# A convolution's totals moved to ScalarE, and two residual sums moved into a TensorE bank, in a hybrid scan kernel

## The chip, the cores and the metric

The kernel runs on one core of one Trainium2 chip. The metric is the device time in microseconds of one execution. PE is TensorE's matmul side and PEld its weight loads, DVE is VectorE, ACT is ScalarE, POOL is GpSimd, SP is SyncE, which issues the DMAs. L769 means line 769 of the kernel before.

## The reference

Eight images of 96 channels by 64x64 pixels pass through two layers. The first is a state-space block with a channel-attention convolution; the second is a linear attention and a feed-forward with rounded numbers. What matters here, cut:

```python
# layer 0, x: (b, 64, 64, 96)
xc = silu(depthwise3x3(in_proj(ln(x))) + conv_b)          # 192 channels
ys = selective_scan(...)          # 4 directions, 16 states, 4096 steps: h = exp(dt*A)*h + dt*u*B; y = C.h
x  = x * skip_scale + out_proj(ln(y) * silu(z))
h  = conv3x3(gelu(conv3x3(ln(x)) + cab1_b)) + cab2_b
a  = sigmoid(relu(h.mean((2, 3)) @ ca1_w.T + ca1_b) @ ca2_w.T + ca2_b)
x  = x * skip_scale2 + h * a
# layer 1, t: tokens of 96
t = t + (q k^T v)(ln(t)) @ Wff + bff                      # no softmax: one matrix per image
t = t + q_acc(q_acc(W2 @ q_mul(relu(q_acc(q_acc(W1 @ q_mul(ln(t))) + b1)))) + b2)
```

`q_mul` rounds to an 8-bit float, `q_acc` to a 16-bit one.

## The kernel before

An image is cut into 8 chunks of T = 512 pixels; a tile is channels by 512. The main loop is the scan. Its `units` are image by pixel order by direction by chunk, 32 to an image, 256 in all. A unit has 24 slots. In each slot ACT makes one 128x512 tile of decays into a bank (`decays`, L1062), two slots ahead; DVE runs one scan over it (L1123) and, in a bit over half of the slots, the product with C (L1125); ACT copies the last column out for the next chunk (the `carry` copies, L1126 and L1131). POOL makes the inputs of four slots at a time (`inputs`, L946, 128x2048) and the products with C that DVE doesn't (`outputs`, L952). PE adds the states up (`sums`, L972), ACT evicts the sum (`gather`, L992). `nat`, `ua`, `ub` (L919 to L928) are the step sizes; `delta`, `du`, `b`, `c` come by DMA on SP's queue.

Instructions stand on each engine in the order in which the Python program issues them (a schedule written out by hand); `plan` names the slot of each step of the scan.

Everything else is run as side work from the same loop. `advance` is called at the end of each slot: it moves `clock` on by one, issues the DMAs that are due (`later` puts one HOLD = 3 slots on), and lets each side stream run one step. A step is a generator that issues some instructions and yields for how many slots it rests: `yield PA` is two slots, for a matmul to end before its eviction is issued; `landed` waits LAND = 11 slots from a fetch. There are two streams: `front` of the next image (kit `f0`), and `back_end` of the image before (kit `f1`), whose stages run in turn: `gated`, `first_conv`, `second_conv`, `channel_gate`, `attention`, `joined`, `feed_forward`. Image 0's units have no back end beside them. After the last unit the back end of image 7, apart from its first stage, runs alone, its chunks dealt to four kits (`f1`, `f0`, `y01`, `y2`): this is the tail. A kit has one bank, `bank(k.tag, ...)`, so each new use of it waits for the eviction of the last.

The stages that the change touches, per chunk:

- `second_conv`: three matmuls (L655) into the bank, ACT adds the bias and writes the tile `t` (L664), DVE sums `t` over its 512 columns into a column of `totals` (L666), and `t` is stored. `channel_gate` (L674) reads `totals` after the last chunk. One chunk's fetch is issued two chunks ahead (`nearer`).
- `feed_forward`: one matmul with the image's joined attention matrix `qkvf` (L767); DVE adds the bank, the bias `bff` and the residual tile `t` into `t` (L769); `norm` centres and scales (L376 to L382: centring matmul, ACT's square and copy, variance matmul, ACT's logarithm and exponential); DVE writes the 8-bit tile (L774); three times a matmul (L778), ACT's conversion and ReLU (L780, L781); ACT's 8-bit tile (L783); three matmuls (L787) with ACT's conversion to 16 bits and bias (L789, L790); POOL adds the result `o16` to `t` (L792), and `t` is stored to `out`.

In the trace an fp32 matmul stands as two records, an fp16 or fp8 one as one.

Of the kernel before, what the change touches and what calls it, by code (L numbers as in the profile page):

```python
# [10 lines left out]
F16 = mybir.dt.float16  # L11
F8 = mybir.dt.float8e5
AF = mybir.ActivationFunctionType
ALU = mybir.AluOpType
AX = mybir.AxisListType
# [4 lines left out]
B, C, HW = 8, 96, 64  # L20
# [18 lines left out]
PA = 2  # L39
# [4 lines left out]
def kernel(ctx: ExitStack, tc: tile.TileContext, a, out):  # L44
# [8 lines left out]
    nc = tc.nc  # L53
# [3 lines left out]
    wp = ctx.enter_context(tc.tile_pool(name="weights", bufs=1))  # L57
# [5 lines left out]
    def bank(tag, name):  # L63
        return psum.tile([P, T], F32, tag=tag, name=name, bufs=BANKS[tag])


    ident = wp.tile([P, P], F32, name="ident")
    make_identity(nc, ident)

    def const(shape, value, name):  # L70
        t = wp.tile(shape, F32, name=name)
        nc.vector.memset(t, value)
        return t
# [27 lines left out]
    for base, mult, step in ((0, 1, -16), (15, -1, 16)):  # L101
        nc.gpsimd.affine_select(
            out=heads, in_=heads, compare_op=ALU.is_ge, fill=0.0, base=base,
# [9 lines left out]
    def later(dst, src):  # L113

        requests.append((clock[0] + HOLD, dst, src))
# [7 lines left out]
    def load(name, shape):  # L123
        return into(wp.tile(shape, F32, name="w_" + name), a[name])
# [43 lines left out]
    cab2_b = load("cab2_b", [C, 1])  # L168
# [5 lines left out]
    wff, bff = load("wff", [C, C]), load("bff", [C, 1])  # L174
# [92 lines left out]
    totals = wp.tile([C, NC], F32, name="totals")  # L267
# [14 lines left out]
    def landed(*parts):  # L282
        while clock[0] < max(p.ready for p in parts):
            yield 1
# [87 lines left out]
    def norm(k, srcs, sq, d):  # L372

        ps = bank(k.tag, "ctr")[:C, :]
        for i, src in enumerate(srcs):
            nc.tensor.matmul(ps, cen_c, src, start=i == 0, stop=i == len(srcs) - 1)  # L376
        yield PA
        nc.scalar.activation(sq, ps, AF.Square)
        nc.scalar.copy(d, ps)  # L379
        yield 1  # L380
        ps = bank(k.tag, "var")[:C, :]
        nc.tensor.matmul(ps, ones_c, sq, start=True, stop=True)  # L382
        yield PA
        inv_std(ps, ps)
        yield 1
        return ps
# [140 lines left out]
    def back_end(b, s):  # L527
# [6 lines left out]
        small = {}  # L534
# [107 lines left out]
        def nearer(p, c):  # L642
            for dy in range(3):
                later(p.t[32 * dy : 32 * dy + 32], mid[:, 8 * c + dy : 8 * c + dy + 8, :])
            p.ready = clock[0] + LAND

        def second_conv(k, cs):
            if not k.solo:
                for p, c in zip(k.m3, cs):
                    nearer(p, c)  # L650
            for n, c in enumerate(cs):
                yield from landed(k.m3[n % 2])
                ps = bank(k.tag, "cab2")[:C, :]
                for dx in range(3):
                    nc.tensor.matmul(  # L655
                        ps, cab2_w[:, dx, :], k.m3[n % 2].t[:, :, dx : dx + HW], start=dx == 0, stop=dx == 2
                    )
                    if dx == 1:
                        yield 1
                yield PA  # L660
                if n + 2 < len(cs):
                    nearer(k.m3[n % 2], cs[n + 2])
                t = (k.s1, k.d1)[n % 2][:C]
                nc.scalar.activation(t, ps, AF.Identity, bias=cab2_b)  # L664
                yield 1
                nc.vector.tensor_reduce(totals[:, c : c + 1], t, AX.X, ALU.add)  # L666
                later(td[:, bass.ts(c, T)], t)
                if n == len(cs) - 1:
                    sources(k, cs[0])
                yield 1  # L670
# [25 lines left out]
        def sources(k, c):  # L696
            for part, src in ((k.ya, td), (k.za, x1d), (k.bs, s["base"])):
                fetch(part, src[:, bass.ts(c, T)])
# [41 lines left out]
        def normed_again(k, n, c):  # L740
            fetch(k.ln, lnd[:, bass.ts(c, T)])
            fetch(k.t2[n % 2], x1d[:, bass.ts(c, T)])
# [18 lines left out]
        def feed_forward(k, cs):  # L761

            for n, c in enumerate(cs):
                t = k.t2[n % 2].t[:C]
                yield from landed(k.ln, k.t2[n % 2])
                ps = bank(k.tag, "att")[:C, :]
                nc.tensor.matmul(ps, small["qkvf"], k.ln.t, start=True, stop=True)  # L767
                yield PA
                nc.vector.scalar_tensor_tensor(t, ps, bff, t, ALU.add, ALU.add)  # L769
                if n + 1 < len(cs):  # L770
                    normed_again(k, n + 1, cs[n + 1])
                yield 1
                rs = yield from norm(k, (t,), k.s1[:C], k.d1[:C])
                nc.vector.tensor_tensor(k.x8, k.d1[:C], rs, ALU.mult, saturate=False)  # L774
                yield 1
                for f in range(3):
                    ps = bank(k.tag, "ff1")
                    nc.tensor.matmul(ps, w1[:, bass.ts(f, P)], k.x8, start=True, stop=True)  # L778
                    yield PA
                    nc.scalar.copy(k.h16[:, f, :], ps)  # L780
                    nc.scalar.activation(k.h16[:, f, :], k.h16[:, f, :], AF.Relu, bias=b1[:, f : f + 1])  # L781
                    yield 1
                nc.scalar.activation(k.h8, k.h16, AF.Copy, saturate=False)  # L783
                yield 1
                ps = bank(k.tag, "ff2")[:C, :]
                for f in range(3):
                    nc.tensor.matmul(ps, w2[:, f, :], k.h8[:, f, :], start=f == 0, stop=f == 2)  # L787
                yield PA
                nc.scalar.copy(k.o16, ps)  # L789
                nc.scalar.activation(k.o16, k.o16, AF.Identity, bias=b2)  # L790
                yield 2
                nc.gpsimd.tensor_tensor(t, t, k.o16, ALU.add)  # L792
                later(out[b, :, bass.ts(c, T)], t)
                yield 1

        chunks = range(NC)[::-1]
        return (
            (gated, chunks), (first_conv, chunks[1::2]), (second_conv, chunks), (channel_gate, None),
            (attention, chunks), (joined, None), (feed_forward, chunks),
        )  # L800

# [423 lines left out]
```

## Time and profile before

| | |
|---|---|
| three runs: median (lowest to highest) | 11345.4 us (11343.77 to 11359.79) |
| the profiled execution: own time | 11372.37 us |
| its span | 11370.7 us |
| granted TensorE clock, share of full | 0.822 |
| first scan starts, last scan ends | 351.7 us, 11092.1 us |
| time of the 32 units of image 0 | 1287.8 us |
| of images 1 to 7 | 1351.2, 1351.7, 1348.8, 1348.3, 1348.2, 1348.3, 1356.1 us |

The profiled execution's own time is 1.7 us more than its span, and 27 us more than the median. Times inside it are told from the span's start. The times of units are taken from the start of their first scan on DVE. Image 0 has no back end beside its units, and images 1 to 6 have both streams, so that the difference of some 61 us is the price of the side work there; image 7 has a second `gated` beside its last units in place of the front stream.

The page gives for each engine the busy time, its share of the span and the count of instructions; a table of stretches gives the same for parts of the span. A group's row gives line, engine, operation, what is written from what, the count, then busy time, the mean in ns of one, and the idle time of the engine just before, with what ended it. Idle time of an engine that isn't the bound costs nothing.

### The profile page before, as it was taken

How to read it: one execution, taken by the hardware profiler on the slowest of the kernel's cores; microseconds unless marked ns; L12 is line 12 of the kernel's file. 1: busy time of each engine (PE TensorE's matmuls, PEld its weight loads, DVE VectorE, ACT ScalarE, POOL GpSimd, SP SyncE). 2: the span in 40 equal slices, each digit the busy share in tenths (PEclk: the TensorE clock that was granted, in tenths of full speed). 3: DMA queues.
4: the chain of work that ended last, by engine and by line, in shares of the span. 5: the costliest groups of instructions: out<-in, count | busy, mean ns of one | idle time of the engine just before them, and what ended most of it. 6: DMA issues, size and time to landing. Idle time of an engine off the chain costs nothing. (4 is left out here: it accounts for less than half of the span.)

```text
span 11370.7 us, 97041 instructions
## 1 busy us (share of the span) xinstructions
PE 8567.3 (75%) x23270; PEld 2328.5 (20%) x23270; DVE 10367.4 (91%) x10828; ACT 7508.4 (66%) x14939; POOL 10398.7 (91%) x2783
## 2 busy tenths in 40 slices
PE   6577657887778877888678876788768887676677
PEld 2111112222122211222112221222212221111122
DVE  0799999999999999999999999999999999999991
ACT  3566656767666676667766676666766667666674
POOL 0799999999999999999999999999999999999990
PEclk8678778888788877889778887888878888787787
DMA  2788878898888888888888888889888888888872
GB/s 71 171 197 197 201 189 210 209 225 196 203 210 212 219 198 202 210 215 215 195 207 210 216 214 194 210 205 228 202 200 211 212 220 195 198 198 195 201 188 78
DMA packets 1081039, 2253.24 MB, mean 198 GB/s; under 512 B 419609, under 2 KB 420314, under 8 KB 949395
## 3 DMA queue, kind: packets, MB, share of 16 engines
q1 hardware_dynamic: 1080467, 2247.05, 81.3%
q8 instruction: 184, 3.01, 0.1%
q14 instruction: 388, 3.18, 0.1%
HBM read 1507.14 MB, written 336.69 MB: 162 GB/s over the span
## 5 line engine op out<-in xcount | busy, mean ns | idle before, releaser
L946 POOL TENSOR_TENSOR hb<-b,du 128x2048 f32<-128x2048 f32 x1536 | 6939.0, 4535 | 21.3 <-DMA du<-ua 14.3
L1062 ACT ACTIVATE da<-delta,w_a_logs 128x512 f32<-128x512 f32 x6144 | 4216.7, 689 | 696.3 <-DVE hb L1123 575.8
L972 PE MATMUL p<-hb,halves 128*64 128x512 f32 x12288 | 3822.7, 731 | 800.1 <-POOL hb L952 382.1
L1123 DVE TENSOR_TENSOR_SCAN da<-da,carry,hb 128x512 f32<-128x512 f32 x3087 | 3949.0, 1279 | 58.0 <-ACT da L1062 54.3
L952 POOL TENSOR_TENSOR hb<-hb,c 128x2048 f32<-128x2048 f32 (+2 forms) x768 | 2984.9, 3887 | 304.7 <-ACT carry L1131 252.2
L1123 DVE TENSOR_TENSOR_SCAN hb<-da,carry,hb 128x512 f32<-128x512 f32 x2289 | 2781.0, 1264 | 57.7 <-ACT da L1062 56.7
L1125 DVE TENSOR_TENSOR hb<-da,c 128x512 f32<-128x512 f32 x3528 | 2440.5, 692 | 154.0 <-DVE da L1123 0.9
L1126 ACT COPY carry<-da 128x1 f32<-128x1 f32 x3528 | 554.9, 157 | 2351.6 <-DVE hb L1125 2341.1
L972 PEld LDWEIGHTS p<-hb,halves 128*64 128x64 f32 x12288 | 916.2, 161 | 3540.7 <-issue 2129.5
L434 PE MATMUL conv<-f0im,taps 97*128 97x512 f32 (+1 forms) x2088 | 903.5, 664 | 95.9 <-ACT f0pre L490 54.3
L928 POOL TENSOR_TENSOR ua<-nat,ua 128x512 f32<-128x512 f32 x256 | 327.3, 1279 | 257.5 <-DMA b<-xd 257.5
L1123 DVE TENSOR_TENSOR_SCAN da<-da,hb 128x512 f32<-128x512 f32 x441 | 537.7, 1219 | 26.0 <-POOL hb L946 24.6
L925 DVE SCALAR_TENSOR_TENSOR nat<-dt,nat 128x512 f32<-128x512 f32 x384 | 259.5, 676 | 238.9 <-ACT nat L923 238.9
L911 PE MATMUL dt<-dts,dt_w 7*64 7x512 f32 (+1 forms) x1024 | 450.0, 657 | 16.9 <-DVE nat L925 12.4
L981 PE MATMUL p<-u,ident 128*128 128x512 f32 x768 | 438.3, 699 | 3.6 <-DMA u<-y 3.6
L376 PE MATMUL ctr<-f1b,cen_c 96*96 96x512 f32 x460 | 271.9, 697 | 193.4 <-DVE f1b L769 158.8
L434 PEld LDWEIGHTS conv<-f0im,taps 97*128 97x128 f32 (+1 forms) x2088 | 254.6, 174 | 681.6 <-issue 523.5
L1123 DVE TENSOR_TENSOR_SCAN hb<-da,hb 128x512 f32<-128x512 f32 x327 | 377.9, 1204 | 4.9 <-ACT da L1062 4.9
L382 PE MATMUL var<-f1b,ones_c 96*96 96x512 f32 x346 | 207.4, 684 | 153.6 <-ACT f1b L379 145.3
L792 POOL TENSOR_TENSOR f1b<-f1b,f1o 96x512 f32<-96x512 f32 x58 | 67.7, 1167 | 252.0 <-ACT f1o L790 251.9
L1131 ACT COPY carry<-hb 128x4 f32<-128x4 f32 (+2 forms) x768 | 146.8, 191 | 197.4 <-DVE hb L1123 184.8
L655 PE MATMUL cab<-f1m,cab_w 96*96 96x512 f32 x348 | 206.0, 719 | 90.9 <-ACT f1b L664 41.4
(416 smaller groups left out, 7710.5 us busy)
## 6 DMA issues: line engine op xcount, KB each, us to landing
b<-xd SPq DMA_DIRECT2D x1024, 512.0 KB
c<-xd SPq DMA_DIRECT2D x1024, 512.0 KB
delta<-nat SPq DMA_DIRECT2D x1536, 128.0 KB
du<-ua SPq DMA_DIRECT2D x1024, 128.0 KB
y<-yt SPq DMA_DIRECT2D x512, 256.0 KB
u<-y SPq DMA_DIRECT2D x384, 256.0 KB
ua<-u SPq DMA_DIRECT2D x256, 256.0 KB
du<-ub SPq DMA_DIRECT2D x512, 128.0 KB
```

What stands on the lines that cost most here:

```text
L376: nc.tensor.matmul(ps, cen_c, src, start=i == 0, stop=i == len(srcs) - 1)
L434: nc.tensor.matmul(ps, taps[:, t, lo : lo + n], im[:, r0 + dy : r0 + dy + 8, dx : dx + HW], start=t == 0, stop=t == 8,)
L911: nc.tensor.matmul(ps, dt_w[32 * w.k : 32 * w.k + R + 1, d], w.dts, start=True, stop=True)
L928: nc.gpsimd.tensor_tensor(x, u.nat, x, ALU.mult)
L946: nc.gpsimd.tensor_tensor(hb, u.bc[0, g], u.du[j].unsqueeze(1).to_broadcast([P, G, T]), ALU.mult)
L952: nc.gpsimd.tensor_tensor(hb, hb, u.bc[1, TILES[n][0]][:, lo:, :], ALU.mult)
L972: nc.tensor.matmul(ps, halves, u.hb[n][:, i, :], start=TILES[n][0] == 0 and m == 0, stop=False, skip_group_check=True)
L981: nc.tensor.matmul(ps, w, x, start=False, stop=True, skip_group_check=True)
L1062: nc.scalar.activation(da[q], u.delta[j], AF.Exp, scale=a_neg[:, u.k, j, g * G + m : g * G + m + 1])
L1123: nc.vector.tensor_tensor_scan(dd if banked else x, dd, x, 0.0 if u.start else col, ALU.mult, ALU.add)
L1125: nc.vector.tensor_tensor(hb[:, m, :], d, u.bc[1, g][:, m, :], ALU.mult)
L1126: kept.append(lambda col=col, d=d, at=first_at: nc.scalar.copy(col, d[:, at : at + 1]))
```

## The change

Three sums are moved. In `second_conv` the DVE instruction that sums the tile goes, and the activation that writes the tile sums it as well, into the same column of `totals`; the step loses one slot. In `feed_forward`, the residual `t` is added by a second matmul with the identity into the bank that holds the attention's product; ACT evicts the bank with the bias `bff`, where DVE added all three. At the end of `feed_forward` the bank is opened once more: one matmul with the fp32 identity for `t`, and one with an fp16 identity for `o16`; ACT copies the sum to `t`, where POOL added them; one slot more goes by. `ident16` is made once at the start.

```diff
     ident = wp.tile([P, P], F32, name="ident")
     make_identity(nc, ident)
+
+    ident16 = wp.tile([C, C], F16, name="ident16")
+    nc.vector.tensor_copy(ident16, ident[:C, :C])
...
                 t = (k.s1, k.d1)[n % 2][:C]
-                nc.scalar.activation(t, ps, AF.Identity, bias=cab2_b)
-                yield 1
-                nc.vector.tensor_reduce(totals[:, c : c + 1], t, AX.X, ALU.add)
+                nc.scalar.activation(t, ps, AF.Identity, bias=cab2_b, accum_out=totals[:, c : c + 1])
                 later(td[:, bass.ts(c, T)], t)
...
                 ps = bank(k.tag, "att")[:C, :]
-                nc.tensor.matmul(ps, small["qkvf"], k.ln.t, start=True, stop=True)
+                nc.tensor.matmul(ps, small["qkvf"], k.ln.t, start=True, stop=False)
+                nc.tensor.matmul(ps, ident[:C, :C], t, start=False, stop=True)
                 yield PA
-                nc.vector.scalar_tensor_tensor(t, ps, bff, t, ALU.add, ALU.add)
+                nc.scalar.activation(t, ps, AF.Identity, bias=bff)
...
                 nc.scalar.activation(k.o16, k.o16, AF.Identity, bias=b2)
-                yield 2
-                nc.gpsimd.tensor_tensor(t, t, k.o16, ALU.add)
+                yield 1
+                ps = bank(k.tag, "out")[:C, :]
+                nc.tensor.matmul(ps, ident[:C, :C], t, start=True, stop=False)
+                nc.tensor.matmul(ps, ident16, k.o16, start=False, stop=True)
+                yield PA
+                nc.scalar.copy(t, ps)
                 later(out[b, :, bass.ts(c, T)], t)
```

## The prediction

> **What bounds the kernel now.** I read the page's busy times first, then a table of stretches cut at the units of the scan (one unit is 24 slots, so 24 scans on DVE), then the groups of the touched lines, then the waits.
>
> ```profile
> span 11370.7 us, 97041 instructions
> PE 8567.3 (75%) x23270; PEld 2328.5 (20%) x23270; DVE 10367.4 (91%) x10828; ACT 7508.4 (66%) x14939; POOL 10398.7 (91%) x2783
> ```
>
> Two engines stand at 91%, DVE and POOL. The unit starts show that the scan runs from 351.7 to 11092.1 us; before and after it both rest. Which of the two binds differs by stage, so I cut stretches. In the order below: image 0, units 14 to 17 and 24 to 31, where no image is yet behind and no back end runs; image 1, units 14 to 17 (second convolution) and 24 to 31 (feed-forward); the same two of image 4; the same two of image 7; and three stretches of the tail.
>
> ```profile
> core 0: us, PE busy (x) PEld busy (x) DVE busy (x) ACT busy (x) POOL busy (x), PEclk, DMA share, GB/s
> 915.85:1036.90 121.05, 77.59 (x202) 20.14 (x198) 116.08 (x119) 78.43 (x155) 120.21 (x32) 0.75 0.87 204
> 1319.52:1599.43 279.91, 167.47 (x468) 48.05 (x464) 272.52 (x278) 164.83 (x344) 279.01 (x74) 0.75 0.79 189
> 2235.36:2365.58 130.22, 97.64 (x245) 26.12 (x245) 123.50 (x132) 87.84 (x170) 120.87 (x33) 0.82 0.89 214
> 2664.59:2950.60 286.01, 204.29 (x530) 51.14 (x530) 281.27 (x292) 215.86 (x431) 285.74 (x81) 0.76 0.82 197
> 6291.31:6417.88 126.57, 99.15 (x267) 25.99 (x264) 123.40 (x133) 82.88 (x165) 120.84 (x33) 0.86 0.92 223
> 6711.52:6999.41 287.89, 201.70 (x534) 51.90 (x534) 281.15 (x292) 216.23 (x431) 286.84 (x81) 0.78 0.82 197
> 10321.96:10450.89 128.93, 87.68 (x214) 23.64 (x212) 123.40 (x133) 72.61 (x152) 120.70 (x33) 0.75 0.83 196
> 10739.01:11051.80 312.79, 230.34 (x557) 60.48 (x557) 293.83 (x310) 225.31 (x453) 288.82 (x81) 0.79 0.80 197
> 11195.00:11230.00 35.00, 23.46 (x52) 8.43 (x52) 5.76 (x10) 11.47 (x15) 0.00 (x0) 0.82 0.39 102
> 11288.00:11333.00 45.00, 31.33 (x64) 10.57 (x65) 9.22 (x14) 33.48 (x53) 4.61 (x4) 0.70 0.16 48
> 11333.00:11371.00 38.00, 16.90 (x38) 5.22 (x36) 2.73 (x4) 32.84 (x52) 4.59 (x4) 0.65 0.09 26
> ```
>
> See three things. Alone, the scan is POOL's: 279.01 of 279.91 us. In the feed-forward of images 1 to 6 POOL is still full (286.84 of 287.89), DVE 5 to 7 us short of full. In the second convolution DVE leads (123.40 of 126.57) and POOL rests 5.7 us or more. So the change takes from DVE where DVE binds, and from POOL where POOL binds. In the tail ACT carries the feed-forward: 32.84 of the last 38 us.
>
> ```profile
> L769 DVE SCALAR_TENSOR_TENSOR f1b<-att,w_bff,f1b 96x512 f32<-96x512 f32 x58 | 42.3, 730 | 23.7 <-PE att L767 23.7
> L666 DVE TENSOR_REDUCE totals<-f1b 96x1 f32<-96x512 f32 x58 | 38.7, 667 | 69.0 <-ACT f1b L664 63.1 <-ACT carry L1126 6.0
> L792 POOL TENSOR_TENSOR f1b<-f1b,f1o 96x512 f32<-96x512 f32 x58 | 67.7, 1167 | 252.0 <-ACT f1o L790 251.9 <-ACT carry L1126 0.2
> L664 ACT ACTIVATE f1b<-cab,w_cab_b 96x512 f32<-96x512 f32 x58 | 38.9, 670 | 27.1 <-PE cab L655 27.1
> L713 ACT COPY f1b<-x 96x512 f32<-96x512 f32 x58 | 33.3, 575 | 37.3 <-PE x L707 36.9 <-DMA du<-ua 0.5
> ```
>
> The 252 us of POOL before L792 are two waits, one of 221.6 us: POOL has nothing to do in the tail. They cost nothing and aren't to be gained.
>
> [...] An eviction that waits for its matmul therefore holds the exponentials behind it. The trace fits: ACT's carry copies wait 2341 us for DVE, with nothing overtaking. [...] L666 has one input, L769's other input lies in a bank. [...] the scan's own bank-and-SBUF product (L1125) lies at 0.68 to 0.70 us throughout. So I count the removed time itself[...]
>
> **The change part by part.** 64 chunks, of which 56 (7 images) run beside the scan, 8 in the tail.
>
> *Second convolution.* Away: 56 DVE reduces of 0.667 = 37.4 us, 5.3 per image. Added: the accumulator's reading on ACT. No row shows it: from 0 (free) to one more small ACT instruction, nearest the 128x1 carry copy, 0.157 us. A gain is excluded, as the activation stays. I take 0.16, 1.3 us of ACT per image, hidden: the ACT work of that stage is 82.88 of 126.57. One slot per chunk goes; since a chunk pair is paced by LAND (14 slots per pair), the stage shrinks only from 52 to 50 slots, and attention starts 2 slots earlier. After the cut, image 4's stretch has DVE 123.4-5.3 = 118.1 plus its 3.2 of idle = 121.3, and POOL 120.84, which in image 0 needs 0.84 more. Two engines this close get in each other's way, so I take 122.2: 4.4 saved, times 4 (images 3 to 6). Images 1, 2 and 7 (130.2, 130.2, 128.9) have more idle that stays, so the full 5.3 goes, times 3. Sum 33.5 us.
>
> *Attention's sum.* Away: DVE's 0.730 per chunk, 5.1 us in units 24 to 31. Added: an fp32 matmul (two records, 1.10 us as a pair in the timeline of the loop) and ACT's Identity with bias, 0.670 as L664.
>
> *Feed-forward's sum.* Away: POOL's 1.167, 8.1 us in seven units. Added: an fp32 matmul of 1.10, an fp16 one (no row; the fp8 rows of the same width take 0.441 and 0.545 us, an fp32 pair 1.10; I take 0.5), and ACT's copy, 0.575 as L713. One slot more per chunk, 26 for 25, so the stage ends 6 slots later: now its last L792 stands in unit 31 at slot 4, then near slot 10, before the image's end, so nothing drains alone. No DMA is added; the store to `out` issues a slot later on SP.
>
> For image 4's units 24 to 31: POOL 286.84-8.1 = 278.7, with image 0's 0.9 of idle 279.6; DVE 281.15-5.1 = 276.0, plus its 6.7 of idle 282.8. Between them, near DVE's side: 282.3, a gain of 5.6; image 1 gives 4.7 likewise. I take 5.3 times 6 = 32. Units 22 and 23 hold one more chunk, 0.73 of DVE, times 7 = 5. Image 7 is DVE's, 5. Sum 42 us.
>
> *What hides the additions.* PE gets 2.7 us per chunk: in seven units 19 on 202 of 288, hidden by PE's 86 us of idle. ACT gets 1.25: 8.7 on 216, hidden in 72 us of idle. But ACT's exponential must be there before its scan. Taking each exponential's end from the start of its scan, in units 22 to 30 of images 1 to 6, it is done a median of 2.2 us before, under 0.7 us in 8 or 9% of slots. 168 added ACT steps of some 0.6 us, a twelfth of them met by no slack: 8 us at most, I take 4. If PE is late at an eviction this cover is gone; that is the rival below. New waits: PE stands at the fp16 matmul until ACT's bias step (L790) is done, with the scan's `sums` behind it, whose tiles POOL then needs; POOL waited for those matmuls only 7.0 us in the whole run.
>
> *Tail.* First round: four more fp32 matmuls ahead of the centring ones [...]: 0.86 to 1.7 us each; 4 us. ACT is full from there: 4 more evictions and 8 copies at about 0.5 of added time, 6. The last POOL add (1.15) is traded for a matmul and a copy. Together +10 (6 to 15). The one cast at set-up is under 0.3 us.
>
> Sum: -33.5 -42 +4 +10 = -62 us. The profiled execution took 11372.4 us, to 11310; it lies 27 us above the median of the runs (11345.4), so against the median: **11283 us**, 0.55% faster.
>
> **Rivals.**
> *A. ACT behind PE (slower).* Both new evictions wait for matmuls two slots back; ACT's FIFO then holds the exponentials and DVE stops. From 62 us of stall, 1.1 per chunk, the gain is gone; at 1.8 us per chunk (one slot) it costs 101: 11384. For it: 115 us of the scan's waits are for `da`, one of 6 us. Against: L789, which stands as close behind its matmuls on the same stream, idled 2.4 us in all, and L664 27, mostly in the tail.
> *B. The second convolution is held by transfers.* Its stretch of image 4 has a DMA share of 0.92, and 4% shorter would want 0.95. Then 33 us fail: 11316. Against: no wait of POOL or DVE there ends in more than a few us on a DMA.
> *C. Stalls move.* Attention is shifted by 2 slots, feed-forward chunks meet other slots of the unit. Stalls of 4 to 6 us in both engines exist (units 17, 19, 22 in different images), and images 1 and 2 lose 3 us to images 3 to 6 with the same program. One such per image, gained or lost: 31 us either way, 11252 to 11314.
> *D. The accumulator isn't free or the adds don't leave.* The lines say they leave; an accumulator of 0.5 us is 28 us of ACT work, mostly hidden.
>
> **How the numbers follow.** A measurement tells about 0.2% from no change, 22.7 us: under 11322.7 is faster, over 11368.1 slower. Chances: forecast 0.52 and C 0.18, both faster; B 0.10, at the edge, 0.06 faster and 0.04 within; A 0.18, mild stalls 0.07 within, a slot's worth 0.11 slower; D 0.02, halved between faster and within. Sums 0.77, 0.12, 0.11. The range takes C on the good side with a margin for the mid-way values (11235) and mild A on the other (11350).
>
> **What would show it.** Right: no L666, L769 or L792 counterparts; the seven feed-forward units near 282 us with POOL near 279 and not full; the three of the second convolution near 122; the tail some 10 us longer. Wrong: DVE's wait for `da` up by tens of us, ACT's new evictions idle for PE by over 0.5 us each, or units 24 to 31 no shorter although POOL rests.

## The result, and the profile after

The changed kernel takes **11372.1 us** (median of 20 runs, 11365.6 to 11379.0), beside 11349.2 us (20 runs, 11332.7 to 11362.4) for the kernel before: a ratio of **1.0020**, 95% interval 1.0013 to 1.0027. It is 23 us slower, where 62 us less were forecast. Lines of the changed kernel stand up to 6 higher than those of before: the scan is L1129 (was L1123), the decays L1068 (L1062), POOL's inputs and outputs L952 and L958 (L946 and L952).

The page's busy times after:

```profile
span 11367.3 us, 97731 instructions
PE 8666.7 (76%) x23590; PEld 2386.4 (21%) x23590; DVE 10314.7 (91%) x10701; ACT 7569.0 (67%) x15131; POOL 10327.7 (91%) x2719
```

DVE has 53 us less work and POOL 71, and the span is that of before. The work left as announced; the time did not. The two profiled executions also differ by an accident of the first: from the last scan to the end it took 278.7 us before and 265.5 after. In the one before, the last chunk of `gated` came 18 us later (its residual sum starts 64.7 us after the last scan, against 47.0), and that execution lies some 20 us above its median. I therefore compare the stretch from the first scan to the last, the **scan period**: 10740.4 us before, **10748.5** after.

The stretches of the profile after, cut at the same units as before (image 1, units 14 to 17 and 24 to 31; image 7, the same two), with the same columns:

```profile
2234.96:2364.01 129.05, 92.82 (x233) 25.50 (x232) 122.00 (x125) 88.20 (x178) 120.66 (x33) 0.83 0.92 222
2663.30:2947.94 284.64, 208.49 (x563) 54.06 (x561) 276.95 (x285) 220.69 (x442) 280.49 (x74) 0.81 0.83 199
10329.39:10456.70 127.31, 86.78 (x215) 23.81 (x215) 121.77 (x125) 73.21 (x161) 120.23 (x33) 0.77 0.84 199
10745.86:11059.46 313.60, 236.04 (x593) 62.52 (x592) 288.89 (x303) 228.97 (x461) 281.78 (x74) 0.83 0.80 196
```

And image 4, units 14 to 17, 17 to 22 and 24 to 31:

```profile
6287.81:6415.69 127.88, 100.32 (x272) 27.34 (x270) 122.11 (x124) 83.48 (x174) 120.30 (x33) 0.85 0.93 225
6415.69:6627.32 211.63, 178.61 (x540) 53.16 (x536) 202.24 (x214) 148.84 (x304) 200.62 (x54) 0.89 0.89 223
6710.74:6998.13 287.39, 217.15 (x574) 56.66 (x572) 276.94 (x285) 219.61 (x441) 281.15 (x74) 0.81 0.82 197
```

In image 4's second convolution DVE does nine instructions fewer than before (124 for 133), the reduces among them, and should have lost 5.3 us; its busy time fell by 1.3, from 123.40 to 122.11, so something in it grew, and the stretch grew too, from 126.57 to 127.88. In its feed-forward POOL and DVE are both full no longer (281.15 and 276.94 of 287.39), and the stretch is as long as before. Something holds the two that is neither of them.

The groups of DVE and ACT that moved:

```profile
L1129 DVE TENSOR_TENSOR_SCAN hb<-da,carry,hb 128x512 f32<-128x512 f32 x2289 | 2786.6, 1265 | 117.5 <-ACT da L1068 112.1 <-ACT carry L1132 4.4
L694 DVE TENSOR_SCALAR dgate<-ident,gate 96x96 f32<-96x96 f32 x8 | 38.0, 4750 | 0.3
L1068 ACT ACTIVATE da<-delta,w_a_logs 128x512 f32<-128x512 f32 x6144 | 4218.0, 690 | 768.0 <-DVE hb L1129 645.4
L667 ACT ACTIVATION_READ_ACCUMULATOR f1b<-cab,w_cab_b 96x1 f32 x58 | 11.2, 193 | 0.0
L796 PE MATMUL out<-f1o,ident 96*96 96x512 f16 x58 | 26.6, 458 | 0.0
L798 ACT COPY f1b<-out 96x512 f32<-96x512 f32 x58 | 33.3, 574 | 14.5 <-PE out L796 14.5
```

The same first three of the kernel before:

```profile
L1123 DVE TENSOR_TENSOR_SCAN hb<-da,carry,hb 128x512 f32<-128x512 f32 x2289 | 2781.0, 1264 | 57.7 <-ACT da L1062 56.7
L693 DVE TENSOR_SCALAR dgate<-ident,gate 96x96 f32<-96x96 f32 x8 | 17.6, 2206 | 0.3
L1062 ACT ACTIVATE da<-delta,w_a_logs 128x512 f32<-128x512 f32 x6144 | 4216.7, 689 | 696.3 <-DVE hb L1123 575.8
```

Two things are to be seen. First, the scans of one form now wait 112.1 us for ACT's decays where they waited 56.7, **and the decays in turn wait longer for DVE** (645.4 for 575.8). ACT's busy time stands at 67%: it isn't overrun, it is held. Second, a 96x96 product of the channel gate, which the change doesn't touch, takes 4750 ns instead of 2206. No other group of DVE that stays in the program grew by more than 6 us.

**The gate's product.** The timeline of the profile before, around it (start, duration, engine, line), in image 4:

```profile
6393.36 9.00 POOL L946 TENSOR_TENSOR hb<-b,du 128x2048 f32<-128x2048 f32 x2
...
6399.94 2.48 DVE L693 TENSOR_SCALAR dgate<-ident,gate 96x96 f32<-96x96 f32 x1
6402.35 1.21 DVE L1123 TENSOR_TENSOR_SCAN hb<-da,hb 128x512 f32<-128x512 f32 x1
```

and of the profile after:

```profile
6389.85 8.97 POOL L952 TENSOR_TENSOR hb<-b,du 128x2048 f32<-128x2048 f32 x2
...
6393.39 5.50 DVE L694 TENSOR_SCALAR dgate<-ident,gate 96x96 f32<-96x96 f32 x1
6398.81 2.32 DVE L1129 TENSOR_TENSOR_SCAN hb<-da,hb 128x512 f32<-128x512 f32 x2
```

Both times the product ends when POOL's pair of 128x2048 products ends: 6393.36 + 9.00 = 6402.36 and 6389.85 + 8.97 = 6398.82. In the tail, where POOL does nothing beside it, it takes 0.27 us. Before, it starts during the second product of a pair and waits out its rest; after, the gate comes two slots earlier, the product starts in the last 0.7 to 1.0 us of the first, and sits through the whole second as well. In all eight profiles that have the product on DVE, each of the seven beside the scan ends 0.06 or 0.07 us after a POOL product does. So it is held until POOL's product is over, 2.48 or 2.49 us long before and 5.24 to 5.50 after, where the hold lasts over a second POOL product as well. What holds it, no trace shows. Seven images times 2.9 us are 20 us of DVE.

**The banks of the decays.** Three banks hold the decays, from a pool of three buffers. In the timeline of the profile after, image 4, unit 14, the scans of slots 12, 13 and 14 (counted from 0), with the decay of slot 13 (what an instruction waited for stands in brackets at the end):

```profile
6308.61 1.27 DVE L1129 TENSOR_TENSOR_SCAN hb<-da,carry,hb 128x512 f32<-128x512 f32 x1
6309.92 0.69 ACT L1068 ACTIVATE da<-delta,w_a_logs 128x512 f32<-128x512 f32 x1 [2.55 <-DVE hb L1129]
...
6310.65 1.28 DVE L1129 TENSOR_TENSOR_SCAN hb<-da,carry,hb 128x512 f32<-128x512 f32 x1 [0.76 <-ACT da L1068]
...
6312.21 2.46 DVE L1129 TENSOR_TENSOR_SCAN hb<-da,carry,hb 128x512 f32<-128x512 f32 x2 [0.28 <-ACT da L1068]
```

The decay at 6309.92 has idled 2.55 us until the scan just ahead of its own was over (6308.61 + 1.27), with two further banks in the pool. Then it takes 0.69 us, and DVE stands 0.76 us for it, and 0.28 once more a scan later, as ACT is late now. The compiled program tells why: it gives this decay the bank of the decay just before it. In a strict rotation each would get the bank of the third before. The bank of the one just before goes to 39 of the 6144 decays in the kernel before, and to **77 in the changed one**. I call these bad banks. By stage, from the compiled programs:

| decays given the bank of the one just ahead | units 0-13 | 14-16, second conv. | 17-21 | 22-23 | 24-30, feed-forward |
|---|---|---|---|---|---|
| before | 23 | 10 | 4 | 1 | 1 |
| after | 23 | 23 | 22 | 7 | 2 |
| totals alone (first experiment) | 23 | 23 | 22 | 7 | 9 |

They sit almost all in slot 13 (34 of 39 before, 70 of 77 after), the second of four slots without a product on DVE, where the scans follow each other at 1.2 us instead of 1.9.

The pool leaves the strict rotation in a second way too: 221 decays before and 235 after get the bank of the second before, and in the traces 127 and 120 of these begin only as the scan two ahead ends. No scan waits for these decays themselves, but they are made later than they could be.

### The profile page after: what moved, and what is told of

Its sections match the earlier page's. It is cut to its first block, busy times and chain, and to the rows that moved or that the text cites. A ratio compares the mean times of both kernels' runs of the same rounds, so it can differ in the third digit from the quotient of the medians.

```text
span 11367.3 us, 97731 instructions
## 1 busy us (share of the span) xinstructions
PE 8666.7 (76%) x23590; PEld 2386.4 (21%) x23590; DVE 10314.7 (91%) x10701; ACT 7569.0 (67%) x15131; POOL 10327.7 (91%) x2719
## 5 line engine op out<-in xcount | busy, mean ns | idle before, releaser
L952 POOL TENSOR_TENSOR hb<-b,du 128x2048 f32<-128x2048 f32 x1536 | 6931.3, 4528 | 34.0 <-PE p L978 17.2
L1068 ACT ACTIVATE da<-delta,w_a_logs 128x512 f32<-128x512 f32 x6144 | 4218.0, 690 | 768.0 <-DVE hb L1129 645.4
L978 PE MATMUL p<-hb,halves 128*64 128x512 f32 x12288 | 3784.1, 727 | 756.9 <-POOL hb L958 357.7
L1129 DVE TENSOR_TENSOR_SCAN da<-da,carry,hb 128x512 f32<-128x512 f32 x3087 | 3949.9, 1280 | 61.6 <-ACT da L1068 54.1
L958 POOL TENSOR_TENSOR hb<-hb,c 128x2048 f32<-128x2048 f32 (+2 forms) x768 | 2980.3, 3881 | 348.9 <-ACT carry L1137 302.1
L1129 DVE TENSOR_TENSOR_SCAN hb<-da,carry,hb 128x512 f32<-128x512 f32 x2289 | 2786.6, 1265 | 117.5 <-ACT da L1068 112.1
L934 POOL TENSOR_TENSOR ua<-nat,ua 128x512 f32<-128x512 f32 x256 | 325.7, 1272 | 259.4 <-DMA b<-xd 257.3
L1129 DVE TENSOR_TENSOR_SCAN da<-da,hb 128x512 f32<-128x512 f32 x441 | 537.0, 1218 | 23.7 <-POOL hb L952 22.6
L1129 DVE TENSOR_TENSOR_SCAN hb<-da,hb 128x512 f32<-128x512 f32 x327 | 378.7, 1203 | 3.7 <-ACT da L1068 3.7
L621 PE MATMUL cab<-f1im,cab_w 97*32 97x512 f32 x1044 | 267.3, 633 | 15.5 <-DMA f1im<-xld 7.4
L929 ACT ACTIVATE nat<-nat,one 128x512 f32<-128x512 f32 x384 | 272.5, 710 | 0.1
```

The source lines that it names most:

```text
L929: nc.scalar.activation(u.nat, u.nat, AF.Ln, bias=one)
L934: nc.gpsimd.tensor_tensor(x, u.nat, x, ALU.mult)
L952: nc.gpsimd.tensor_tensor(hb, u.bc[0, g], u.du[j].unsqueeze(1).to_broadcast([P, G, T]), ALU.mult)
L958: nc.gpsimd.tensor_tensor(hb, hb, u.bc[1, TILES[n][0]][:, lo:, :], ALU.mult)
L978: nc.tensor.matmul(ps, halves, u.hb[n][:, i, :], start=TILES[n][0] == 0 and m == 0, stop=False, skip_group_check=True)
L1068: nc.scalar.activation(da[q], u.delta[j], AF.Exp, scale=a_neg[:, u.k, j, g * G + m : g * G + m + 1])
```

## The experiments

Each ratio is to the kernel before, run beside the experiment. Theory: the sums are worth about what was forecast, and two things took it back, the banks' order and the gate's product. Rival: ACT and PE, with the new steps, are late by themselves (the forecast's rival A), or a part is worth nothing.

**Each part alone.** Part 1 alone:

```diff
-                nc.scalar.activation(t, ps, AF.Identity, bias=cab2_b)
-                yield 1
-                nc.vector.tensor_reduce(totals[:, c : c + 1], t, AX.X, ALU.add)
+                nc.scalar.activation(t, ps, AF.Identity, bias=cab2_b, accum_out=totals[:, c : c + 1])
```

> The kernel before with the first part of the change alone: the second convolution's totals summed by ACT as it writes, one slot less per chunk. Theory [...]: in the compiled program each exponential of the scan is given one of three banks, and it should be the one used three exponentials ago; in the kernel before 39 of 6144 are given the bank of the exponential just before (so ACT must wait for the scan that reads it, 0.76 us of DVE each), in the changed kernel 77, in this one 84. So +45 x 0.76 = +34 us; the gate's tensor_scalar waits for POOL as in the changed kernel, +20; the removed reduces give -33: together some +20, 11370 us. Rival (ACT stands behind PE at the new evictions): this part adds no eviction, so the full relief of 33 us should come: 11316 us.

Measured 11383.6 us, ratio 1.0031 (1.0019 to 1.0042): 35 us slower, 14 more than the theory's sum, and the rival's 11316 is far off. This third, with the least work added anywhere, loses more by itself than the whole change. Its gate product took 5.2 to 5.5 us, as in the whole change.

The attention's sum alone:

```diff
-                nc.tensor.matmul(ps, small["qkvf"], k.ln.t, start=True, stop=True)
+                nc.tensor.matmul(ps, small["qkvf"], k.ln.t, start=True, stop=False)
+                nc.tensor.matmul(ps, ident[:C, :C], t, start=False, stop=True)
...
-                nc.vector.scalar_tensor_tensor(t, ps, bff, t, ALU.add, ALU.add)
+                nc.scalar.activation(t, ps, AF.Identity, bias=bff)
```

> The kernel before with the attention's sum alone made in the bank (identity matmul, ACT evicts with the bias, DVE's three-operand add gone). No slot is added or taken, and the compiled program gives the scan's exponentials the very same banks as before (39 of the bank just before). Theory: DVE loses 0.73 us x 56 = 41 us in units where POOL binds as much, so only some 10 us come, the tail adds 5: about 11344 us, between 11330 and 11350; the gate's tensor_scalar stays at 2.5 us. Rival (ACT behind PE): the new eviction costs over 0.4 us of stall per chunk, 11365 us or more.

Measured 11337.1 us, 0.9991 (0.9985 to 0.9998): a little faster, within the theory's range. Its bank order is that of before, step for step, and its gate product still takes 2.5 us.

The feed-forward's last sum alone:

```diff
-                yield 2
-                nc.gpsimd.tensor_tensor(t, t, k.o16, ALU.add)
+                yield 1
+                ps = bank(k.tag, "out")[:C, :]
+                nc.tensor.matmul(ps, ident[:C, :C], t, start=True, stop=False)
+                nc.tensor.matmul(ps, ident16, k.o16, start=False, stop=True)
+                yield PA
+                nc.scalar.copy(t, ps)
```

> The kernel before with the feed-forward's last sum alone made in the bank (two matmuls, ACT copies, POOL's add gone, one slot more per chunk). Banks: 44 exponentials of the bank just before, against 39, +4 us. Theory: POOL loses 65 us in all, in units where DVE is full but for 1 us per unit, so 10 to 20 us come, the tail adds 3 to 5: about 11342 us. Rival (ACT behind PE): 11365 us or more.

Measured 11373.0 us, 1.0022 (1.0015 to 1.0030): 25 us slower; the theory missed here, and the figure is what rival A named. Its scan period is 14.9 us longer: 18.0 us in the units 24 to 30, where it has 6 bad banks and the kernel before 1, and a little shorter elsewhere. The parts alone add up to some 50 us, the whole change lost 23: they don't simply add.

**The gate's product on ACT**, with all three parts:

```diff
-            nc.vector.tensor_scalar(dgate, ident[:C, :C], gate, None, ALU.mult)
+            nc.scalar.activation(dgate, ident[:C, :C], AF.Identity, scale=gate)
```

> The changed kernel with one more edit: the channel gate's diagonal (the identity times the gate) written by ACT instead of DVE's tensor_scalar. The scan's banks are those of the changed kernel, one by one. Theory [...]: that DVE instruction, 0.27 us alone, took 5.2 to 5.5 us in each of images 0 to 6's back ends since it waited for two POOL products in a row; without it DVE is free 7 x 5.1 = 36 us earlier, of which the bank waits leave most: about 11342 us. Rival (the wait of DVE there is covered, as ACT and POOL are behind anyway): 11368 to 11374 us, as the changed kernel.

Measured 11321.5 us, 0.9975 (0.9965 to 0.9985). The row of the profile of this kernel:

```profile
L694 ACT ACTIVATE dgate<-ident,gate 96x96 f32<-96x96 f32 x8 | 2.9, 362 | 0.4 <-DVE gate L693 0.4
```

Seven waits of 5.2 to 5.5 us gave way to 0.36 us on ACT, and the kernel came down by 51 us, more than their 38. The trace has 38 us of it in units 14 to 16 of images 1 to 7, where the product stands. One line that the change doesn't touch turns a loss into a gain.

**The banks by number**, in the kernel before, in the changed kernel, and each with the gate's product on ACT:

```diff
-    BANKS = {"da": 3, ...
+    BANKS = {"da0": 1, "da1": 1, "da2": 1, ...
...
-        da[q] = bank("da", "da")
+        da[q] = bank(f"da{q % 3}", "da")
```

> The kernel before, with each unit step's exponential given its bank by number (step modulo 3) where before a pool of three hands them out. In the program before, 39 of 6144 exponentials get the bank of the scan just ahead and start only when it has ended; DVE then stands 0.76 us. Theory (the hand-out of banks costs the scan): all 39 stalls go, 39 x 0.76 = 30 us, so about 11319. Rival (ACT is late in those slots whatever bank it has): no change, 11348.

Measured 11291.2 us, 0.9956 (0.9942 to 0.9970): 50 us off the kernel before.

> The changed kernel, banks of the exponentials fixed by number. In the program of the changed kernel 77 exponentials get the bank of the scan just ahead. Theory: 77 x 0.76 = 58 us go, from 11372 to about 11314, DVE's wait for the exponentials falling from 116 to under 65 us. Rival (ACT is late anyway): 11372.

Measured 11264.8 us, 0.9931 (0.9918 to 0.9943): some 100 us off the changed kernel.

> The changed kernel, banks fixed by number and the gate's 96x96 product made by ACT. The gate alone brought it to 11321. Theory (two separate causes, which add): 11321 - 58 = 11263. Rival (the gate's relief already let ACT catch up, the banks are immaterial): 11321.

Measured 11222.3 us, 0.9894 (0.9881 to 0.9908).

> The kernel before, banks fixed by number and the gate's product made by ACT, the three sums left as they were. Theory: 30 us for the banks and 7 x 2.2 = 15 us for the gate, 11303; the three sums are then worth the rest of the way to the changed kernel with the same two edits. Rival (the sums are worth nothing): the same time as that kernel.

Measured 11278.5 us, 0.9941 (0.9929 to 0.9954).

All four went where the theory sent them, the banks further: 50 us for 39 bad banks and 100 for 77 are 1.3 us each, where I had counted only the 0.76 of the first stall. That is a quotient, not the price of one: stage by stage the gain doesn't follow the count. In images 1 to 7 numbering took 7.6 us from units 22 and 23 of the kernel before, which have no bad bank there, and 11.3 from units 24 to 30 of the changed kernel, which have one. It also does away with the second departure from the rotation, and no run separates the two kinds. The same slot of the kernel with fixed banks (image 4, unit 14, all three parts):

```profile
6262.61 4.80 DVE L1129 TENSOR_TENSOR_SCAN hb<-da,carry,hb 128x512 f32<-128x512 f32 x4
6262.92 0.21 ACT L1132 COPY carry<-da 128x1 f32<-128x1 f32 x1
6263.18 1.44 ACT L1068 ACTIVATE da<-delta,w_a_logs 128x512 f32<-128x512 f32 x2
```

Four scans (slots 12 to 15) stand without a gap, and two decays are made while the first two run. The groups of that kernel with the gate on ACT as well, which answer to those above:

```profile
L1129 DVE TENSOR_TENSOR_SCAN hb<-da,carry,hb 128x512 f32<-128x512 f32 x2289 | 2773.2, 1264 | 39.0 <-ACT da L1068 35.8 <-ACT carry L1132 2.1
L1068 ACT ACTIVATE da<-delta,w_a_logs 128x512 f32<-128x512 f32 x6144 | 4225.0, 689 | 504.7 <-DVE hb L1129 380.4 <-DMA delta<-nat 3.9 <-DMA td<-f1b 1.0
L958 POOL TENSOR_TENSOR hb<-hb,c 128x2048 f32<-128x2048 f32 (+2 forms) x768 | 2983.4, 3885 | 227.3 <-ACT carry L1137 194.8 <-PE p L987 14.9 <-PE dt L917 4.4
```

The wait for decays is down from 112.1 to 35.8 us; POOL's wait for the carry copies, which stand in ACT's queue behind the decays, from 302.1 (the changed kernel) to 194.8. The banks alone bring the two to 35.7 and 238.4, the gate alone to 111.9 and 254.8. That second wait may be why a bad bank costs more than its own stall; it isn't tested apart.

The change between kernels with the same edits, as a quotient of the two ratios:

| the kernel otherwise | without the change | with it | quotient | us |
|---|---|---|---|---|
| as it is | 1 | 1.0020 | 1.0020 | +23 |
| banks fixed | 0.9956 | 0.9931 | 0.9975 | -28 |
| banks fixed, gate on ACT | 0.9941 | 0.9894 | 0.9953 | -53 |

The last quotient lies between 0.9927 and 0.9979 by the ends of the two intervals, -83 to -24 us. The middle one, reckoned likewise, between 0.9948 and 1.0001, -59 to +1 us. The 76 us between the first and the last line are the two causes; taken in this order, 51 the banks, 25 the gate. The scan periods of the single profiles also make 76 us, and give 45 and 31. Taken in the other order the split could differ: the kernel before with only the gate's product on ACT wasn't run.

**The parts alone, with banks fixed and gate on ACT.**

> The kernel before with fixed banks and the gate's product on ACT (11279), and of the change its first part alone: the second convolution's totals by ACT's accumulator. Alone on the kernel before, this part lost 35 us. Theory [...]: with both out of the way it gains the forecast 33 us, 11246. Rival (the accumulator's reading or the earlier attention costs by itself): 11279 or more.

Measured 11228.3 us, 0.9895 (0.9881 to 0.9908): against 0.9941, a quotient of 0.9954, -52 us, more than the theory's 33.

> The kernel before with fixed banks and the gate on ACT (11279), and the attention's last sum alone in the bank. POOL stays full in the feed-forward units, so by the forecast's stage account only units 22 and 23 and image 7 gain: about 10 us, 11269. Rival (DVE binds there after all): the whole of its 56 x 0.65 = 36 us, 11243.

Measured 11258.1 us, 0.9920 (0.9907 to 0.9934): -24 us, of which the scan period shows 18. That lies between the theory's 10 and the rival's 36.

> The kernel before with fixed banks and the gate on ACT (11279), and the feed-forward's last sum alone in the bank. DVE is not relieved, so by the stage account no more than a few us in the loop, and the tail's 6 us are lost: 11277 to 11287. Alone on the kernel before, this part lost 25 us. Rival (its matmuls and copies push the exponentials late by themselves, banks or not): 11300 or more.

Measured 11278.3 us, 0.9939 (0.9926 to 0.9951): nothing either way. The scan period has 1.4 us less. So of the 25 us that this part lost alone, nearly all went with the banks and the gate, although its units 24 to 30 are still 5.0 us longer in sum. ACT idles for the new matmuls about as long here (13.1 us) as in the kernel with this part alone (14.3), so that idling by itself isn't what cost the 25 us.

The totals, alone +35, are now worth more than forecast, and as much as the whole change (0.9894). The last two parts together take 24 us more out of the scan period (10620.5 to 10596.8) and give 13 of it back in the tail (261.5 to 275.0).

**The relief without the shift:** the totals on ACT, the slot kept.

```diff
+                nc.scalar.activation(t, ps, AF.Identity, bias=cab2_b, accum_out=totals[:, c : c + 1])
+                yield 1
```

> The kernel before with the totals by ACT's accumulator, but with the slot that the reduce had kept empty, so that nothing after it moves. In its program 53 exponentials get the bank of the scan just ahead (39 before, 84 where the slot goes as well). Theory [...]: the gate's product stays at 2.5 us, the relief of 33 us shows less some 11 us for 14 more bad banks: about 11325. Rival (the relief itself turns into waits): as with the slot removed, 11380.

Measured 11340.3 us, 0.9993 (0.9984 to 1.0001). The rival falls: what lost 35 us with the slot gone loses nothing with the slot kept. The theory hoped for 15 us more. Counted afterwards, with the quotient of 1.3 us per bad bank, the 14 more cost 18, and the gate's product, at 3.0 to 3.3 us, another 5, which leaves 33 - 18 - 5 = 10 of gain, and 9 were measured; with a price fitted to other runs, the agreement may be luck. All 14 more lie in units 14 to 16. So the shift isn't needed for bad banks: to take one instruction out of the program already changes what the pool hands out.

## Why the prediction was wrong

**The step that failed is the one that put what happens around the change at nothing.** The sum had relief, added work, and under "What hides the additions" 4 us for ACT's slack. It had no term for the order in which the program gives out the decays' banks (51 us by the times, 45 by the scan periods), nor for where the gate's product falls once attention comes two slots earlier (25 and 31 us); rival C saw the shift of two slots, as 31 us either way, and not the banks. The scan period makes the sum: forecast -71.5, and with both removed measured -68.0 (10664.8 to 10596.8), but +8.1 as it stood.

**The slack of ACT** was taken over all units and slots together: done a median of 2.2 us ahead, late in 8 or 9% of slots. That hid where the lateness sits. In the trace before, the median in slots 14 and 15 is 0.7 and 0.8 us, and in 34 of 256 units the decay of slot 13 begins only as the scan ahead ends. Beside ACT's 66% busy, the row of L1062 with 575.8 us of waiting for DVE was in view; I read it as ACT having time to spare. With the banks fixed in the kernel before, that wait is 410.2 us: some 166 of it were ACT held by a bank given out of turn.

**The removed time**: "I count the removed time itself" looked at the inputs of the two DVE instructions that go; of L792, GpSimd's own, it said nothing. The one at stake was an instruction that stayed. A 96x96 product at 2206 ns, where a 97x97 one (L735) takes 248, was in the profile before, a sign that I passed over.

**Second convolution, -33.5**: near in size once clean. Units 14 to 16 of images 1 to 7 are 28.9 us shorter in the kernel with all parts than in the one without, banks fixed and gate on ACT in both; image 4, forecast 4.4, gave 4.7 (123.19 to 118.45). One reduce frees 0.59 us, not 0.667: in the trace before the next instruction starts that much after it. The rows of image 4, in the columns of the tables above, first without the change (units 14 to 16 and 24 to 30):

```profile
6261.58:6384.77 123.19, 98.41 (x272) 25.98 (x268) 120.80 (x132) 84.16 (x167) 119.54 (x33) 0.86 0.93 223
6675.33:6962.90 287.57, 201.54 (x534) 51.70 (x534) 281.01 (x291) 217.25 (x433) 286.51 (x81) 0.78 0.82 196
```

and with it (units 14 to 16, 17 to 21 and 24 to 30):

```profile
6219.65:6338.10 118.45, 100.48 (x272) 27.67 (x270) 116.07 (x123) 85.48 (x177) 117.56 (x33) 0.87 0.94 227
6338.10:6543.57 205.47, 175.49 (x538) 52.90 (x536) 201.42 (x213) 148.66 (x302) 201.63 (x54) 0.90 0.95 236
6624.96:6912.18 287.22, 216.93 (x572) 56.63 (x571) 276.73 (x284) 220.19 (x441) 281.11 (x74) 0.79 0.82 197
```

**Feed-forward, -42**: too large, by 15 even when clean: units 22 to 31 gave -26.8 (9.2 in 22 and 23, 17.6 later). The forecast carried DVE's idle of 6.7 us over unchanged. In image 4's last row above DVE has 276.73 of 287.22, so it idles 10.5 (without the change, 6.6). By the profile's waits, averaged over images 3 to 6, 4.0 us for decays where the same kernel without the change has 2.4, and new waits of about 1.1 for the 8-bit tile's scale on ACT. Images 3 to 6 so gained 0.3 to 1.6 us each instead of 5.6, images 1, 2 and 7 had 3.4 to 5.0 (units 24 to 30). This is rival A in small, some 3 us per image instead of 0.6 for ACT's lateness.

**Not in the sum**: units 17 to 21 gained 18.7 us, 14.9 of it with part 1 alone. DVE's and POOL's work there is the same, and part 1 touches these units only by moving attention two slots: stalls went, on this reading. This is rival C's mechanism on its good side, and it covered for the feed-forward; units 0 to 13 got 6.7 us longer. So that the total of -68 agrees with -71.5 is luck.

**Tail, +10**: right within the scatter. From the last scan to the end, kernels with all three parts took 263.6 to 275.0 us (four profiles, mean 267.4), those with none, besides the disturbed one, 257.3 and 264.0: +7. The reading of the accumulator, taken as 0.16 us, is 0.193 us, a separate record, and holds ACT for 0.09 (the next ACT instruction starts 0.66 us after the activation did, 0.57 before); the fp16 matmul, taken as 0.5, is 0.458; ACT's copy, taken as 0.575, is 0.574.

**Rivals.** A, slower through ACT behind PE, rests on ACT keeping its order, and the trace before shows it: from the start of unit 24 the next 426 ACT records have one order in images 3 to 6. A gave nearly the right time, and all three signs that the prediction named for being wrong came: DVE's wait for decays rose from 116 to 171 us, ACT's eviction L771 idles 41.3 us for PE over 58 chunks, 0.71 each (L798 14.5, 0.25 each), and the feed-forward got no shorter in images 3 to 6. Yet they don't point at A alone. With banks fixed and the gate on ACT the two evictions idle as long (41.7 and 16.5 us), and the change gains 53 us; and part 1, which adds no eviction, lost 35 by itself. C, stalls that move, came nearest in kind: its bad side is the gate's product. B is refuted: the convolution's stretch did shorten at a DMA share of 0.94, and the next one ran at 0.95. D: the sums did leave.

**Open.** Why the pool hands out a bank just used: the compiled programs show that it does and where, not the rule. How the loss by the banks divides between the bad ones and those of the second kind. Why part 3 alone lost as much as 25 us with only five more bad banks: its gate product takes 2.5 us as before, in its units 24 to 30 48 decays begin only as the scan two ahead ends, against 31 in the kernel before, and fixing banks and gate took nearly all of the loss away; whether the banks alone would have wasn't tried.

The best version seen is the changed kernel with banks fixed and the gate's product on ACT: 11222.3 us, 1.06% under the kernel before. Part 1 alone with the same two edits (11228.3) can't be told from it, by 0.9895 against 0.9894.

## What to carry to other kernels

Before adding up what an edit removes, look for what stands between two full engines: when both wait for a third that is itself waiting for one of them, follow the buffer, and read from the compiled program which buffer each use got. Here a pool of three wasn't a ring of three; name the buffers by number where a lead of two steps is counted on. And look for the few instructions whose duration is many times that of their like: they can be waits in disguise, and a shift of the schedule, also one that only removes work, can change them, as here from 2.5 to 5.5 us.

## What the runs showed that was not expected

- A 96x96 fp32 tensor-and-scalar product on DVE took 0.27 us with GpSimd idle and up to 5.5 us beside two GpSimd 128x2048 products in a row in the changed kernel, ending 0.06 or 0.07 us after the second of them. The mean of its eight was 4.75 there, and 5.47 with banks fixed (all three parts, gate on DVE).
- A decay held by its bank until the scan ahead of its own ended cost DVE some 0.7 us at once (0.76 in the one shown); giving the banks by number took off 50 and 100 us, 1.3 us for each such decay of the program, though not all of it need be theirs.
- The accumulator of an activation is read out by a record of its own, 193 ns for 96x1; it overlaps its activation, and holds ACT for 0.09 us.
- DVE's instructions overlap by about 0.08 us in the trace: a 0.667 us reduce holds DVE for 0.59.
